# A twelve-layer decoder on one core: one transfer for the maxima of half a sequence, and another order and two queues for the rows of the last softmax layer

## The chip, the cores and the metric

The kernel runs on one core of one Trainium2 chip. The metric is the device time of one execution in microseconds, as the median of several runs. A core has engines that each work through their own program in order: TensorE (matrix products; its weight loads are listed apart, as PEld), VectorE (DVE), ScalarE (ACT), GpSimd (POOL) and SyncE (SP), which here only issues transfers. ScalarE and GpSimd can issue transfers too. Engines wait for each other through semaphores; a wait holds everything that stands behind it in that engine's program.

## The reference

The model has four blocks of three layers over x of 8 sequences, 256 positions and 128 features. Each layer is `x = x + f(layernorm(x))`. Softmax attention with 16 heads of 8 features is f in five layers: L0_attn and L1_attn (causal self-attention with rotary positions), L0_xattn and L1_xattn (cross-attention to a context, with masks) and L3_xattn (cross-attention, no mask). The other layers are three mixtures of experts with sorted tokens (L0, L1, L2), channel attention and retention (L2), a state-space scan (L3_attn) and a latent mixture (L3_ffn). The last block, cut:

```python
def _L3_xattn_ref(query, key, value, Wq, bq, Wk, bk, Wv, bv, Wo, bo):
    Q = proj(query, Wq, bq, Sq)          # (8, 16 heads, 256, 8)
    K = proj(key, Wk, bk, Skv)
    V = proj(value, Wv, bv, Skv)
    scores = jnp.einsum('bhqd,bhkd->bhqk', Q, K) / SCALE
    attn = jax.nn.softmax(scores, axis=-1)
    out = jnp.einsum('bhqk,bhkd->bhqd', attn, V)
    ...
    return jnp.einsum('bsd,ed->bse', out, Wo) + bo
...
x = x + _L2_ffn_ref(_layernorm(x, axis=-1), ...)      # experts
x = x + _L3_attn_ref(_layernorm(x, axis=-1), ...)     # state space
x = x + _L3_xattn_ref(_layernorm(x, axis=-1), ctx_1024, ctx_1024, ...)
x = x + _L3_ffn_ref(_layernorm(x, axis=-1), ...)
```

The query of L3_xattn comes from the norm of x; its key and value come from the context, which is there from the start.

## The kernel before

**Two passes of softmax.** A job is one sequence in one softmax layer: 8 sequences x 5 layers, 40 jobs. Pass 1 (`pass1`) multiplies q by k with q's positions on the partitions, 512 columns at a time, and VectorE takes the negative maximum over k (`neg`, line 824). Pass 2 (`pass2`) multiplies again with k's positions on the partitions, ScalarE takes the exponential (`prob`, line 901), and TensorE multiplies by v (`av`, line 873). The maximum is subtracted inside the second product: q's operand has three extra rows that hold it, against rows of ones in k's operand.

**Rows of q and k.** `qs` and `ks` are the operands, [128 rows, 16 heads, 2 sequences x 256 positions] in bf16, two buffers each, one for even and one for odd pairs of sequences. Each fp32 value of q and k is split on GpSimd into three bf16 pieces (`pieces`, lines 647 and 651: cast, subtract, cast, subtract), and all nine products of pieces are contracted: 72 rows. `spread` (lines 655 to 664) writes them with nine transfers per operand (line 661), for each piece three, every one 8 rows of 16 KB, 128 KB. The destination's rows take the 128 partitions of the piece, head by head. `queues` lists the issuing engines: transfer r of a piece goes to queue r modulo their number; with one queue, the generator yields an estimated 2 us after each piece. Only the first pair of the whole kernel uses two queues, SyncE and ScalarE.

**Fronts.** `front` (lines 673 to 752) prepares a pair of sequences: k's projection from the context (cross-attention), wait for the layer before, norm, transposes, q's projection, a wait for pass 2 of the two jobs that used the same buffers two pairs ago (`before`), then k's rows, q's rows, and v. The first wait, at line 678, takes only the first of these two jobs.

**Maxima.** At the end of half a job (8 heads) GpSimd splits `neg` into three pieces `mp` [128 positions, 2 tiles, 3 pieces, 8 heads] (lines 831 to 834). `all_maxima` (lines 838 to 855) transposes this in one matmul to 48 rows of 128 positions, ScalarE copies them to `mT`, and two transfers, one per tile of 128 positions, write 24 rows each into q's three extra rows (line 852). Pass 2 of this half waits for both.

**Order.** All stages are Python generators. `drive` advances pass 1 and pass 2 job by job, and the others (`fronts`, `all_maxima`, `backs`, the expert and scan layers, called aside) when their estimated due time comes; `yield us(t)` gives such an estimate, and a generator that waits for a key in `done` is passed over. What comes out is one fixed program per engine. So a changed estimate or a changed wait can also move other instructions. SyncE's program holds the row transfers, the maxima's transfers, the expert weights (`r_w`, line 1432, 592 KB each), the sorted tokens (lines 1439 and 1467) and the output.

**Around the last softmax layer.** The experts of L2_ffn for the second half of the batch (lines 1462, 1492, 1495, 1497) run while L3_xattn begins on the first half. When they are done, the scan (L3_attn, lines 1611 to 1767) runs on the second half beside L3_xattn of the first; then L3_xattn of the second half runs beside L3_ffn. The layer object `L3x` is L3_xattn; its jobs are the last eight, pairs 0 and 1 the first half, 2 and 3 the second.

Of the kernel before, what the change touches and what calls it, by code (L numbers as in the profile page):

```python
# [11 lines left out]
BF16 = mybir.dt.bfloat16  # L12
# [6 lines left out]
P = 128  # L19
B = 8  # L20
S = 256
T = S // P
D = 128
H = 16
# [5 lines left out]
KM = P - NPC  # L30
# [217 lines left out]
def kernel(  # L248
# [11 lines left out]
    nc = tc.nc  # L260
# [18 lines left out]
    def sb(shape, tag, bufs, dt=F32):  # L279
        return pools["soft"].tile(list(shape), dt, tag=tag, name=tag, bufs=bufs)  # L280
# [29 lines left out]
    def mm_tile(dt=F32):  # L310

        spare[1] += 1
        if spare[0] and spare[1] % 2:
            return ps_s1.tile([P, 512], dt, tag="s1", name="s1")
        return ps_mm.tile([P, 512], dt, tag="mm", name="mm")
# [6 lines left out]
    def bc(ap, axis, n):  # L322

        a = ap.unsqueeze(axis)
        shape = list(a.shape)
        shape[axis] = n
        return a.to_broadcast(shape)
# [10 lines left out]
    def us(t):  # L338
        return t / TICK
# [3 lines left out]
    def wait(*keys):  # L343
        while not done.issuperset(keys):
            yield BLOCKED
# [118 lines left out]
    identb = cpool.tile([P, P], BF16, name="identb")  # L464
# [16 lines left out]
    qss = [cpool.tile([P, H, 2 * S], BF16, name=f"qs{i}") for i in range(2)]  # L481
    kss = [cpool.tile([P, H, 2 * S], BF16, name=f"ks{i}") for i in range(2)]
# [27 lines left out]
    rt_at, n = {}, 0  # L510
# [68 lines left out]
    def layernorm(dst, src, n):  # L579

        st = sb_all([P, n, 6], "ln_st", 8)
        mv = sb_all([P, n, 2], "ln_mv", 8)
        rs = sb_all([P, n], "ln_rs", 8)
        for i in range(n):
            nc.vector.bn_stats(st[:, i, :], src[:, i, :])
            nc.vector.bn_aggr(mv[:, i, :], st[:, i, :])
        inv_root(rs, mv[:, :, 1], n, 1e-5)
        yield us(5)
        for i in range(n):
            one = nc.vector.tensor_scalar(  # L590
                dst[:, i, :], src[:, i, :], mv[:, i, 0:1], rs[:, i : i + 1], ALU.subtract, ALU.mult)
        last.setdefault("dve", one)
        yield us(2.5)
# [41 lines left out]
    def main_line(jobs, loads, aside):  # L635
# [5 lines left out]
        def pieces(src, nm):  # L641

            out, rest = [], src
            for i in range(NPC):
                if i:
                    r = sb([P, 2 * S], "qkf", 3) if i < NPC - 1 else sb([P, 2 * S], f"pc{i}", 2, BF16)
                    nc.gpsimd.tensor_tensor(r, rest, out[-1], ALU.subtract)
                    rest = r
                if i < NPC - 1:
                    b = sb([P, 2 * S], f"pc{i}", 2, BF16)  # L650
                    nc.gpsimd.tensor_copy(b, rest)  # L651
                    out.append(b)
            return out + [rest]

        def spread(dst, pcs, of_q, queues):


            for a, t in enumerate(pcs):
                for r in range(NPC):
                    at = a * NPC + r if of_q else r * NPC + a  # L660
                    queues[r % len(queues)].dma_start(  # L661
                        dst[at : KR : NPC * NPC].rearrange("d h c -> d (h c)"), t)
                if len(queues) == 1:
                    yield us(2)
# [8 lines left out]
        def front(j, y, b):  # L673
            p = b // 2
            if y is L3x:
                yield from wait("L3x")
            before = [("p2", i) for i in (j - 4, j - 3) if i >= 0]
            yield from wait(("w", y.step), ("rows", p % 2), *before[:1])
            if y.w is None:
                y.w = loaded[y.step]  # L680
                if not y.rope:
                    y.bqs = sb([P, 1], "bqs", 2)
                    nc.vector.tensor_scalar(y.bqs, y.w["bq"], scale, None, ALU.mult)
            w = y.w

            def rows_of(n, src):
                f = sb([P, 2 * S], "qkf", 3)
                if y.rope:
                    parts = []
                    for sw, tab in (("", "cos"), ("s", "sin")):  # L690
                        pp = mm_tile()
                        mm(pp, w["w" + n + sw], src, start=True, stop=True)
                        o = sb([P, 2, S], "probw", 4)
                        pv = pp.rearrange("p (b s) -> p b s", b=2)
                        table = bc(rope[tab + n], 1, 2)
                        if "b" + n in w:
                            nc.vector.scalar_tensor_tensor(o, pv, w["b" + n + sw], table, ALU.add, ALU.mult)
                        else:
                            nc.vector.tensor_tensor(o, pv, table, ALU.mult)
                        parts.append(o)  # L700
                        yield us(1)
                    nc.gpsimd.tensor_tensor(
                        f.rearrange("p (b s) -> p b s", b=2), parts[0], parts[1], ALU.add)
                else:
                    pp = mm_tile()
                    mm(pp, w["w" + n], src, start=True, stop=True)
                    if n == "q":
                        nc.scalar.activation(f, pp, AF.Identity, bias=y.bqs, scale=scale)
                    else:
                        nc.scalar.activation(f, pp, AF.Identity, bias=w["bk"])  # L710
                    yield us(1)
                return pieces(f, n)

            first = j == 0
            if y.cross:
                yield from wait(("ctx", p))
                kp = yield from rows_of("k", ctxP[p])
            yield from wait(*y.needs(p))
            x = xp[p]
            xn = sb([P, 2 * T, D], "xn", 1)  # L720
            yield from layernorm(xn, x, 2 * T)
            xnT = sb([P, 2 * S], "xnT", 1)
            one = transpose_to(xnT, xn, 2 * T, nc.scalar.copy)
            if first:
                last["act"] = one
            yield
            if not y.cross:
                kp = yield from rows_of("k", xnT)
                if first:
                    yield from spread(kss[p % 2], kp, False, (nc.sync, nc.scalar))  # L730
            qp = yield from rows_of("q", xnT)
            if "bo" in w:
                nc.gpsimd.tensor_tensor(x, x, bc(w["bo"], 1, 2 * T), ALU.add)
            yield from wait(*before)
            if not first:
                yield from spread(kss[p % 2], kp, False, (nc.sync,))
            yield from spread(qss[p % 2], qp, True, (nc.sync, nc.scalar) if first else (nc.sync,))
            yield us(1)
            kvT = ctxP[p] if y.cross else xnT
            for i in range(2):  # L740
                pv = mm_tile()
                for t in range(T):
                    at = i * S + t * P
                    mm(pv[:, t * D : (t + 1) * D], kvT[:, at : at + P], w["wv"], start=True, stop=True)
                v = vpads[(2 * p + i) % 4]
                for t in range(T):
                    v_in = pv[:, t * D : (t + 1) * D].rearrange("p (h d) -> p h d", h=H)
                    if "bv" in w:
                        nc.vector.tensor_tensor(v[:, t, :, 0:DK], v_in, w.grid("bv", H), ALU.add)
                    else:  # L750
                        nc.vector.tensor_copy(v[:, t, :, 0:DK], v_in)
                yield us(3)
# [85 lines left out]
        def all_maxima():  # L838

            n = NPC * H // 2  # L840
            for j in range(len(jobs)):
                for half in range(2):
                    yield from wait(("mp", j, half))
                    yield us(3.5)
                    mp, q, h0, c0 = maxima.pop(0)
                    pm = mmb_tile()
                    nc.tensor.transpose(pm[: T * n, :P], mp.rearrange("p t r h -> p (t r h)"), identb)
                    mT = sb([T * n, P], "mT", 2, BF16)
                    nc.scalar.copy(mT, pm[: T * n, :P])
                    for t in range(T):  # L850
                        qt = c0 + t * P
                        nc.sync.dma_start(
                            q[KM:, h0 : h0 + H // 2, qt : qt + P], mT[t * n : (t + 1) * n])
                    done.add(("max", j, half))
                    yield 0

# [920 lines left out]
    L3x = Layer("L3_xattn", pair_of("L3_attn"), cross=True)  # L1777
# [70 lines left out]
```

## Time and profile before

| | |
|---|---|
| runs, us | 1732.77, 1742.9, 1731.68; median 1732.77 |
| profiled execution | 1729.58 us, span 1727.8 us |
| TensorE busy | 1435.5 us (83%), 10546 matmuls |
| TensorE's weight loads | 894.7 us (52%) |
| VectorE busy | 952.3 us (55%) |
| ScalarE busy | 615.9 us (36%) |
| GpSimd busy | 608.6 us (35%) |
| TensorE's mean granted clock | 0.914 |
| chain that ended last, by engine | PE 57%, POOL 11%, DVE 11%, issue 8%, DMA 7%, ACT 3%, SPq 2% |

The span runs from the first to the last instruction of the profiled execution. Busy times of engines overlap, so they don't add up to the span. The chain is followed back from the last instruction, at each step to what released it; "issue" in it is time in which an engine waited for nothing that the profile shows, SPq is SyncE's queue. Lines L1 to L1847 are those of the kernel before. TensorE's clock is granted by a throttle and is given as a share of full speed.

The page lists the transfers that the change touches: `ks<-pc` and `qs<-pc` with 177 issues each of 128 KB on SyncE and three each on ScalarE, and `qs<-mT` with 160 issues of 6 KB on SyncE.

### The profile page before, as it was taken

What the parts mean: (1) busy time and instruction counts of PE and PEld (TensorE: products, weight loads), DVE (VectorE), ACT (ScalarE), POOL (GpSimd) and SP (SyncE); (2) the same over time, 40 slices, a digit from 0 to 9 for tenths busy, and PEclk for the clock granted to TensorE, in tenths of its full rate; (3) what the DMA queues carried; (4) which work ended last, traced back from release to release, by engine and by line L of the source; (5) the groups of instructions that cost most, each with busy time, mean ns of one, the idle gap of its engine ahead of it and who ended that gap; (6) DMA issues with size and microseconds to landing.
All of it is one profiled execution on the core that took longest, in us unless ns stands there. A gap on an engine that the chain in (4) does not pass through costs nothing.

```text
span 1727.8 us, 28942 instructions
## 1 busy us (share of the span) xinstructions
PE 1435.5 (83%) x10546; PEld 894.7 (52%) x10546; DVE 952.3 (55%) x2546; ACT 615.9 (36%) x1267; POOL 608.6 (35%) x859
## 2 busy tenths in 40 slices
PE   3897898888799778889989899567967787988997
PEld 1454454566345456545556566356744563554553
DVE  5445776636467553656544455313367355757753
ACT  0352343441333343234443345112322224533551
POOL 3424656412565441252331322312134523342211
PEclk7899999999999899999999999679978888998996
DMA  3332111344201226211245300147400452012000
GB/s 106 90 111 61 40 57 30 112 142 136 72 24 47 66 80 192 89 57 57 58 137 179 113 28 2 57 151 240 146 15 25 148 158 82 11 53 78 8 8 13
DMA packets 113519, 141.64 MB, mean 82 GB/s; under 512 B 12384, under 2 KB 97888, under 8 KB 113248
## 3 DMA queue, kind: packets, MB, share of 16 engines
q1 hardware_dynamic: 94064, 121.33, 22.4%
q10 hardware_dynamic: 16240, 12.17, 2.4%
q0 software_dynamic: 3072, 6.30, 1.1%
q8 instruction: 83, 1.36, 0.3%
q14 instruction: 60, 0.49, 0.1%
HBM read 79.53 MB, written 12.06 MB: 53 GB/s over the span
## 4 chain that ended last, share of the span: by engine, by line
PE 57%; POOL 11%; DVE 11%; issue 8%; DMA 7%; ACT 3%; SPq 2%; another core or an unknown queue 0%; POOLq 0%; ACTq 0%; DVEq 0%
PE av L873 9%; PE sc L1492 6%; PE s L815 6%; PE sc L893 6%; DVE neg L824 4%; PE mm L1462 3%; DMA qs<-pc 2%; PE s L821 2%; PE sc L898 2%; POOL probw L906 2%; SPq L661 2%; POOL r_x L1514 2%; POOL xsorted L1409 2%; PE mm L502 2%; DMA r_w<-in_w_L_big_dram 2%
## 5 line engine op out<-in xcount | busy, mean ns | idle before, releaser
L824 DVE TENSOR_REDUCE neg<-s 128x2 f32<-128x512 f32 (+1 forms) x576 | 387.1, 683 | 217.3 <-PE s L818 78.3
L901 ACT ACTIVATE prob<-sc 128x512 f32<-128x512 f32 x576 | 336.2, 597 | 379.2 <-PE sc L898 196.8
L815 PE MATMUL s<-ks,qs 125*128 125x256 bf16 (+1 forms) x1280 | 236.4, 274 | 89.6 <-DVE neg L824 56.2
L893 PE MATMUL sc<-qs,ks 128*128 128x256 bf16 (+1 forms) x1280 | 227.7, 269 | 4.6 <-DMA qs<-mT 4.3
L815 PEld LDWEIGHTS <-qs 125*128 125x128 bf16 x1280 | 113.5, 102 | 197.5 <-issue 154.4
L1492 PE MATMUL sc<-r_xT,r_w 128*128 128x128 f32 x720 | 166.1, 323 | 46.6 <-ACT r_h L1495 13.8
L873 PE MATMUL av<-prob,vpad 128*32 128x256 f32 (+1 forms) x2048 | 168.3, 368 | 15.9 <-issue 9.8
L1492 PEld LDWEIGHTS sc<-r_xT,r_w 128*128 128x128 f32 x720 | 115.2, 203 | 98.3 <-ACT r_h L1495 44.9
L893 PEld LDWEIGHTS <-ks 128*128 128x128 bf16 x1280 | 110.8, 100 | 97.4 <-issue 65.2
L1497 DVE TENSOR_SCALAR r_h<-sc,r_w 128x128 f32<-128x128 f32 x180 | 62.6, 349 | 157.7 <-PE sc L1492 156.2
L1495 ACT ACTIVATE r_h<-sc,r_w 128x128 f32<-128x128 f32 x180 | 66.1, 368 | 171.6 <-PE sc L1492 143.1
L651 POOL CAST pc<-qkf 128x512 bf16<-128x512 f32 x80 | 51.8, 648 | 209.7 <-ACT qkf L710 148.7
L1462 PE MATMUL mm<-r_w,r_h 128*128 128x128 f32 x600 | 106.9, 292 | 0.8 <-DVE r_h L1497 0.7
L906 POOL TENSOR_TENSOR probw<-prob,sideT 128x512 f32<-128x512 f32 x64 | 84.3, 1318 | 48.7 <-ACT prob L901 48.4
L831 POOL CAST mp<-neg 128x16 bf16<-128x16 f32 x80 | 19.8, 247 | 222.1 <-DVE neg L824 205.7
L1462 PEld LDWEIGHTS mm<-r_w,r_h 128*128 128x128 f32 x600 | 88.7, 203 | 7.4 <-DVE r_h L1497 2.4
L873 PEld LDWEIGHTS av<-prob,vpad 128*32 128x32 f32 x2048 | 47.0, 108 | 87.1 <-issue 55.6
L577 POOL TENSOR_TENSOR ln_rs<-ln_rs,nhalf 128x4 f32<-128x4 f32 x40 | 43.3, 1085 | 131.0 <-DVE ln_rs L576 130.3
L878 ACT COPY avs<-av 128x512 f32<-128x512 f32 x80 | 46.9, 586 | 82.6 <-PE av L873 60.8
L1514 POOL DMA_INDIRECT r_x<-ysorted,r_sloti x48 | 46.5, 970 | 74.6 <-PE s L1477 59.9
L873 PE MATMUL av<-probw,vpad 128*32 128x256 f32 x512 | 53.0, 399 | 23.6 <-POOL probw L906 23.4
L906 DVE TENSOR_TENSOR probw<-prob,sideT 128x512 f32<-128x512 f32 x64 | 56.2, 878 | 27.6 <-ACT prob L901 18.1
(408 smaller groups left out, 2579.0 us busy)
## 6 DMA issues: line engine op xcount, KB each, us to landing
r_w<-in_w_L_big_dram SPq DMA_DIRECT2D x60, 578.0 KB
ks<-pc SPq DMA_DIRECT2D x177, 128.0 KB
qs<-pc SPq DMA_DIRECT2D x177, 128.0 KB
r_w<-in_w_L_big_dram SPq DMA_DIRECT2D x30, 579.0 KB
r_x<-xsorted SPq DMA_DIRECT2D x18, 256.0 KB
ysorted<-r_y SPq DMA_DIRECT2D x18, 256.0 KB
mi<-in_mask_dram ACTq DMA_DIRECT2D x16, 256.0 KB
qs<-mT SPq DMA_DIRECT2D x160, 6.0 KB
```

The source lines that it names most:

```text
L651: nc.gpsimd.tensor_copy(b, rest)
L815: one = mm(bank[:, a, :], q[:KM, g + a, c0 + qt * P : c0 + (qt + 1) * P], k[:KM, g + a, c0 : c0 + nk], start=a == 0 or y.bare, stop=y.bare)
L824: last["dve"] = nc.vector.tensor_reduce(neg[:, qt, g - h0 : g - h0 + nh], bank, AX.X, ALU.max, negate=True)
L873: mm(o, sumsel if sums else v[:, at : at + G], probs[j][0 if sums else 1], start=kt == 0 and not sums, stop=kt == T - 1 and sums == (sideT ...
L893: one = mm(bank[:, a, :], k[:, g + a, c0 + kt * P : c0 + (kt + 1) * P], q[:, g + a, c0 + q0 : c0 + S], start=a == 0 or y.bare, stop=y.bare)
L901: last["act"] = nc.scalar.activation(p, bank, AF.Exp)
L906: eng.tensor_tensor(pw, p, bc(sideT[:, kt, :], 1, nh), ALU.mult)
L1462: mm(py, hid[:, f, :], wt[:, w2 : w2 + D], start=f == 0, stop=f == NF - 1)
L1492: mm(o, wt[:, f * P : (f + 1) * P], xT[:, i, :], start=True, stop=True)
L1495: nc.scalar.activation(hid[:, f, :], o, AF.Relu, bias=bias)
L1497: nc.vector.tensor_scalar(hid[:, f, :], o, bias, 0.0, ALU.add, ALU.max)
L1514: nc.gpsimd.indirect_dma_start(yg[:, i, :], None, ysort, bass.IndirectOffsetOnAxis(ap=sloti[:, at : at + 1], axis=0))
```

## The change

For the maxima, `mp` is transposed in two matmuls, one per tile of 128 positions, side by side into the same bank: 24 rows of 256 positions instead of 48 rows of 128. ScalarE copies 24 x 256, and one transfer writes all 256 positions into q's three extra rows.

For L3x, k's rows are spread right after k's projection, ahead of the wait for the layer before and of the norm; the wait for both earlier pass 2's (`before`) comes ahead of this, so also ahead of the norm. And k's and q's rows of L3x go by two queues: of three transfers per piece, two on SyncE and one on ScalarE. With two queues `spread` gives no estimates between pieces.

```diff
             first = j == 0
+            queues = (nc.sync, nc.scalar) if first or y is L3x else (nc.sync,)
             if y.cross:
                 yield from wait(("ctx", p))
                 kp = yield from rows_of("k", ctxP[p])
+                if y is L3x:
+                    yield from wait(*before)
+                    yield from spread(kss[p % 2], kp, False, queues)
             yield from wait(*y.needs(p))
...
             yield from wait(*before)
-            if not first:
-                yield from spread(kss[p % 2], kp, False, (nc.sync,))
-            yield from spread(qss[p % 2], qp, True, (nc.sync, nc.scalar) if first else (nc.sync,))
+            if not first and y is not L3x:
+                yield from spread(kss[p % 2], kp, False, queues)
+            yield from spread(qss[p % 2], qp, True, queues)
...
                     mp, q, h0, c0 = maxima.pop(0)
                     pm = mmb_tile()
-                    nc.tensor.transpose(pm[: T * n, :P], mp.rearrange("p t r h -> p (t r h)"), identb)
-                    mT = sb([T * n, P], "mT", 2, BF16)
-                    nc.scalar.copy(mT, pm[: T * n, :P])
                     for t in range(T):
-                        qt = c0 + t * P
-                        nc.sync.dma_start(
-                            q[KM:, h0 : h0 + H // 2, qt : qt + P], mT[t * n : (t + 1) * n])
+                        nc.tensor.transpose(
+                            pm[:n, t * P : (t + 1) * P], mp[:, t].rearrange("p r h -> p (r h)"), identb)
+                    mT = sb([n, S], "mT", 2, BF16)
+                    nc.scalar.copy(mT, pm[:n, :S])
+                    nc.sync.dma_start(q[KM:, h0 : h0 + H // 2, c0 : c0 + S], mT)
                     done.add(("max", j, half))
```

In the instruction order of the changed program, as it is built, SyncE has 80 maxima transfers instead of 160, and of L3x's 72 row transfers 48; ScalarE has the other 24. For the first pair of L3x SyncE's program has six transfers of k, then three expert weights, then six of q, then further weights.

## The prediction

> **What bounds the kernel now.** I read the page first: TensorE is busy 1435.5 us of a span of 1727.8 (83%) and carries 57% of the chain that ended last. So a change counts either by TensorE work on that chain or by a stretch in which TensorE stands. I looked for such stretches with the busy time by stretch (columns: stretch, its us, then busy us and instructions of PE, PEld, DVE, ACT, POOL, then granted clock, DMA share, GB/s).
>
> ```profile
> 1355.00:1376.00 21.00, 18.52 (x120) 14.47 (x118) 8.69 (x24) 7.22 (x17) 9.54 (x11) 1.00 0.52 158
> 1376.00:1398.00 22.00, 12.20 (x52) 9.97 (x51) 3.58 (x12) 2.06 (x5) 0.00 (x0) 0.69 0.62 176
> 1397.00:1428.00 31.00, 27.44 (x179) 21.20 (x180) 23.40 (x58) 8.40 (x21) 10.91 (x19) 0.94 0.47 152
> 1428.00:1455.00 27.00, 16.68 (x132) 8.04 (x131) 12.54 (x32) 11.69 (x25) 10.40 (x20) 0.81 0.37 114
> 1455.00:1533.00 78.00, 75.79 (x586) 44.13 (x584) 56.69 (x148) 47.16 (x98) 23.36 (x35) 1.00 0.06 17
> 1533.00:1549.00 16.00, 12.15 (x63) 8.29 (x63) 7.88 (x25) 4.09 (x8) 11.82 (x16) 1.00 0.25 75
> 1570.00:1678.00 108.00, 106.49 (x756) 56.90 (x757) 72.44 (x220) 59.04 (x113) 21.41 (x39) 0.98 0.08 25
> ```
>
> In 1376 to 1398 TensorE idles 9.8 us, its clock is 0.69 and GpSimd does nothing: transfers bound this stretch. In 1455 to 1533 and from 1570 on TensorE is 97% and 99% busy: there only work counts. The chain of waits names the transfer (start, us, what):
>
> ```profile
> 1375.60 0.61 SPq L661
> 1376.31 9.27 DMA qs<-pc
> 1385.60 11.38 DMA qs<-pc
> 1396.98 0.72 issue
> ```
>
> The first pass 1 of L3x starts at 1397.70, when its q rows are in. SyncE's timeline shows why they are late (columns: start, us, queue, line, what, count):
>
> ```profile
> 1359.12 0.77 SPq L661 DMA_DIRECT2D ks<-pc  x1
> 1363.56 4.13 SPq L1432 DMA_DIRECT2D r_w<-in_w_L_big_dram  x3
> 1367.73 3.57 SPq L661 DMA_DIRECT2D ks<-pc  x5
> 1374.27 1.94 SPq L661 DMA_DIRECT2D ks<-pc  x3
> 1376.31 2.47 SPq L661 DMA_DIRECT2D qs<-pc  x3
> 1381.11 6.53 SPq L661 DMA_DIRECT2D qs<-pc  x6
> ```
>
> One k transfer goes out, three expert weights block the queue until 1367.7, eight k transfers follow, and only then q, whose pieces GpSimd had finished at 1372.9. The maxima's rows by their tile (ns min/median/max):
>
> ```profile
> L852 SPq DMA_DIRECT2D qs<-mT x160: 697/722/832, 48.7 to 1662.1; - x160
> L849 ACT COPY mT<-mm x80: 243/254/262, 48.4 to 1661.0; 48x128 bf16<-48x128 bf16 x80
> L847 PEld LDWEIGHTS <-mp x80: 98/99/115, 48.1 to 1660.3; 128*48 128x48 bf16 x80
> L847 PE MATMUL mm<-identb,mp x80: 216/237/303, 48.1 to 1660.3; 128*48 128x128 bf16 x80
> ```
>
> The sum is made against this execution: 1729.58 us, 1.8 of them around the span. It lies 0.2% under the median of the runs, 1732.77; I add the result to the median.
>
> **The change, part by part.**
>
> The maxima, 80 halves (8 sequences, 5 layers, 2 halves). (a) 80 SyncE issues of 0.72 us go, 58 us of queue time; almost all of it lies beside SyncE's waits for the copy itself (356 us for ScalarE's mT in the queue's waits). On the chain, followed stretch by stretch, the landing of a maxima transfer stands three times (2.17, 2.97, 4.62 us), each right behind the first issue of its pair, so it is the second transfer that is awaited; 3 x 0.72 = 2.2 us are saved; ends: 0, and 8 x 0.72 = 5.8 for the eight places where the issue itself is on the chain. What is late next there is the copy, which I cost below. (b) 80 transposes are added on TensorE. The trace has no second one behind a first; one takes 0.17 us from its start to the next instruction (1427.33 to 1427.50), its weight load 0.099. I take 0.11, near the weight load, since back-to-back bf16 matmuls of this kernel start 0.11 apart. L847 lies on the chain at 54 of its 80 places: 54 x 0.11 = +5.9; ends: 0, if TensorE would wait for something else anyway, and 54 x 0.17 = 9.2. (c) The copy goes from 48x128 at 0.254 to 24x256; the nearest row, a 128x256 copy on ScalarE, takes 0.37. That is 80 x 0.116 = 9.3 us of ScalarE, which carries 3% of the chain: +0.3, covered by an engine busy 36%; uncovered it would be 9.3. Together +4.0.
>
> L3x, four pairs of sequences, 18 row transfers each. (d) The k rows of the first pair now stand in SyncE's order ahead of the three weights, six on SyncE and three on ScalarE's queue; q's six and three follow these weights with nothing of k between. Nothing of k leaves between 1367.7 and 1376.2, so q can go as its pieces appear, from 1369.8. The 9.8 us of idling in 1376 to 1398 consist of two waits for weights (3.66 and 3.93), 0.96 for q and small ones. I let one weight wait remain: the three weights now go after k's third piece (1363.4 and two issues, 1.1 us later than 1363.56) and behind eight more transfers of 128 KB (1.05 MB at that stretch's 158 GB/s, 6.6 us). So 9.8 - 3.7 = 6.1 saved; ends 0 (bytes bound it) and 9.8. (e) The clock was 0.69 there against 0.94 in the stretch behind; at 0.9 the 12.2 us of work would take 9.4: 2.8 saved, and 0 at the other end. Late next are the experts: in the changed order 74 pass-1 matmuls, 18 of pass 2 and 12 value matmuls stand ahead of the last expert matmul, against 48, 4 and 0. The experts' end hardly moves; the gain is cashed in 1455 to 1533, which has less softmax work left.
>
> (f) ScalarE now issues 24 transfers. The first of each three waits for GpSimd's first piece, the last for its third, so ScalarE's queue is held from cast to last subtraction: 3.75 us for q (1369.11 to 1372.86), 4.92 for k (1358.46 to 1363.38), plus 0.62 per issue. Behind it stand the experts' r_h in the first pair, for which TensorE waits in program order, and ss_m in the third. I charge one hold of the first pair less what the remaining weight wait absorbs, +3; ends: 0, and 8 holds of 4.3, 35 us. In the second pair 42 pass-1 matmuls stand in a row beside the holds: 21 reductions of 0.68 on VectorE, 14 us of cover; without it, two holds, 8.6 us. (g) The new wait for both earlier pass 2's ahead of the norm costs nothing for pairs 0 and 1, whose buffers are long free, nor for pair 2, where q's projection stood behind all of pass 2 already (128 of 128 matmuls before and after); its cover gone, it would be one norm and projection, 1525.8 to 1535.3, 9.5 us. (h) From pair 2 on, moving three issues of 0.61 off SyncE saves at most 1.8 of q's last landing, and by the rows below 0.2; I take 1.2. Against that, four scan groups that ran while q was on its way (1535 to 1545) now stand behind pass-1 matmuls; VectorE bounds pass 1 there (18.8 of 21 us in 1549 to 1570), so TensorE has gaps for them: +1.5, ends 0 and all of their matmuls, 6.5 (four times 1.1 and two value steps of 1.05). Together -6.1 - 2.8 + 3 - 1.2 + 1.5 = -5.6.
>
> The trace has both forms of (h): nine q transfers by two queues at the start took 10.4 us from first issue to last landing (26.94 to 37.3), by one queue in pair 2 10.6 (1537.96 to 1548.6); both are paced by GpSimd's pieces. The Trainium skill, page "DMA: Bandwidth & Descriptors", section "Issuing engines are not separate DMA queues", speaks against the edit: transfers from any engine end on the same 16 DMA engines, so a second issuer saves issue time alone. By it (h) would be 1.8 and the sum -2.2; by the rows' difference, 0.2, it would be -0.6.
>
> The other softmax layers keep their row order but for a few neighbours. Sum: 4.0 - 5.6 = -1.6, so 1729.58 becomes 1728.0 and the median 1731; I say 1730.
>
> **The rivals.**
>
> Rows really early (20%). q lands by about 1384, 1378 for the last issue after the holds plus six of landing as in the 4.5 to 6.6 us rows of calmer stretches. Pass 1 starts 13.7 us earlier, and all of it arrives at the end; with (h) at 1.8 and the maxima at -2.2 + 0.3 (transposes hidden) that is -17.4: 1715. For: 9.8 us of idling and GpSimd at 0.00. Against: the order puts 26 pass-1 matmuls more ahead of the experts, and pair 2 waits for the scan, not for pass 1.
>
> Bytes bound it (20%). The weights and rows of 1355 to 1398 are the same bytes on the same engines; DMA share 0.52 and 0.62 speaks against, waits for weights on TensorE for. Then (d) and (e) go: -1.6 + 8.9 = +7.3: 1740.
>
> Slower: ScalarE held (15%). One mechanism, (f): ScalarE's in-order queue waits for GpSimd at eight places; six have no pass-1 cover, 6 x 4.3 = 26 in place of 3. With the rest -4.6 that gives +21: 1754. It decides from the point where more than about three holds are uncovered. For: the r_h and ss_m right behind. Against: ScalarE did 2.06 us in 1376 to 1398.
>
> The change not doing what it says: both parts stand in the built order, 80 maxima transfers for 160 and k ahead of the weights; I leave that out.
>
> **How the numbers follow.** My forecast has 45%, 1722 to 1738 by (a) to (c). About 1% is what a measurement here tells from no change, 17 us. Faster by it: most of the first rival and the forecast's tail, 0.17. Slower: the last rival, and a tail of the bytes' case, 0.15. Within: 0.68. The range takes in the first rival's 1715 less 2 and most of the slow one: 1713 to 1750.
>
> **What would show it.** Right: the q landing at 1376 to 1397 gone from the chain, ks issued in one run ahead of three weights, TensorE's idling in that stretch under 5 us; 80 maxima transfers, the copy near 0.37, two L847-type transposes about 0.11 apart; TensorE busy up 8 to 14 us by transposes. Wrong: r_h or ss_m waiting 4 us behind ScalarE's issues, an L3x that starts pass 1 at 1394 or later, or a shift of several us ahead of 1340, where only the maxima part acts and I allow +3.

## The result, and the profile after

The changed kernel takes 1763.33 us in the median of four runs (1753.69 to 1766.64), the kernel before 1734.02 (1731.68 to 1742.9). The ratio is 1.0142, with a 95% interval from 1.0109 to 1.0176: 19 to 31 us slower, where 1730 was forecast and 1750 was the upper end of the range. The span of the profiled execution is 1760.5 us against 1727.8.

Up to L3x the changed kernel is ahead: ScalarE copies the first k projection of L3x (`qkf`, line 710) at 1351.7 us against 1357.6. (In the fourteen traces that have the new maxima part this point lies between 1345.0 and 1357.6 us, so a lead of 5.9 is within the scatter.) All of the loss lies behind this point: from there to the end of the span the changed kernel takes 408.8 us, the kernel before 370.2. The busy time by stretch, for the stretches shown of before and one more (stretch, its us; busy us and instructions of PE, PEld, DVE, ACT, POOL; granted clock, DMA share, GB/s):

```profile
1355.00:1376.00 21.00, 12.94 (x68) 11.21 (x69) 3.47 (x11) 4.94 (x12) 5.92 (x7) 0.79 0.53 167
1376.00:1398.00 22.00, 17.84 (x109) 14.68 (x109) 13.38 (x40) 4.69 (x12) 5.86 (x10) 0.89 0.56 180
1397.00:1428.00 31.00, 21.60 (x96) 14.66 (x96) 17.64 (x33) 4.09 (x10) 7.44 (x19) 0.68 0.37 113
1428.00:1455.00 27.00, 25.84 (x209) 16.77 (x212) 8.89 (x25) 14.38 (x31) 3.93 (x4) 0.99 0.35 101
1455.00:1533.00 78.00, 68.50 (x468) 37.30 (x462) 49.57 (x126) 41.67 (x85) 23.07 (x39) 0.89 0.10 30
...
1551.00:1567.00 16.00, 5.12 (x22) 2.79 (x21) 3.11 (x12) 1.37 (x2) 7.21 (x9) 0.73 0.42 122
1570.00:1678.00 108.00, 97.23 (x634) 56.16 (x632) 76.50 (x220) 43.88 (x85) 26.32 (x51) 0.91 0.08 27
```

The windows stand at the same times in both kernels, though the changed one is 5.9 us further on in its work. The stretch that the change aims at, 1376 to 1398, idles 4.2 us on TensorE instead of 9.8. But the stretch ahead of it idles 8.1 instead of 2.5, the one behind it 9.4 instead of 3.6, with 96 matmuls instead of 179 and a clock of 0.68 instead of 0.94. And at 1551 there is a hole of 11 us.

**First place, the experts.** ScalarE's timeline (start, us, engine or queue, line, what, count; in brackets the idle time ahead and what ended it):

```profile
1353.23 4.89 ACTq L661 DMA_DIRECT2D ks<-pc  x3
1358.18 0.62 ACT L1498 ACTIVATE r_h<-sc,r_w 128x128 f32<-128x128 f32 x2 [5.28 <-DMA ks<-pc]
...
1370.36 3.76 ACTq L661 DMA_DIRECT2D qs<-pc  x3
1374.30 0.62 ACT L1498 ACTIVATE r_h<-sc,r_w 128x128 f32<-128x128 f32 x2 [4.64 <-DMA qs<-pc]
...
1414.36 0.37 ACT L1498 ACTIVATE r_h<-sc,r_w 128x128 f32<-128x128 f32 x1 [14.33 <-PE sc L1495]
```

Three issues hold ScalarE's queue for 4.89 and 3.76 us, since each stands until GpSimd has its piece, and `r_h` of the experts comes behind them. The last line is another matter: there ScalarE waits 14.33 us for an expert matmul. TensorE's timeline shows the first hold, and then what stands ahead of that matmul:

```profile
1358.60 0.80 PE L1495 MATMUL sc<-r_xT,r_w 128*128 128x128 f32 x2 [4.71 <-ACT r_h L1498]
...
1409.13 1.18 PE L819 MATMUL s<-ks,qs 125*128 125x256 bf16 x4 [0.24 <-DVE neg L828]
1410.49 1.19 PE L819 MATMUL s<-ks,qs 125*128 125x256 bf16 x4 [0.18 <-DVE neg L828]
1411.86 1.18 PE L819 MATMUL s<-ks,qs 125*128 125x256 bf16 x4 [0.18 <-DVE neg L828]
1412.84 0.63 PE L1495 MATMUL sc<-r_xT,r_w 128*128 128x128 f32 x2
```

From 1399.2 on, 42 pass-1 matmuls stand in a row, paced by VectorE's reductions (two matmuls per 0.68 us), and the expert comes behind the last. The last tokens leave the experts at 1447.14 us: 95.4 us behind k's projection, where it was 70.7.

**Second place, the scan of pair 3.** TensorE's timeline again, and then VectorE's and GpSimd's:

```profile
1553.75 1.10 PE L706 MATMUL mm<-ctxT,w 128*128 128x512 f32 x2
1565.36 1.01 PE L819 MATMUL s<-ks,qs 125*128 125x256 bf16 x4 [10.51 <-DMA ks<-pc]
1566.73 1.26 PE L819 MATMUL s<-ks,qs 125*128 125x256 bf16 x4 [0.35 <-DVE neg L828]
1567.83 1.22 PE L1740 MATMUL sc<-ss_u,w_L_tables 128*128 128x256 f32 x2
```

```profile
1565.98 0.69 DVE L828 TENSOR_REDUCE neg<-s 128x2 f32<-128x512 f32 x1 [11.66 <-PE s L819]
1566.59 0.16 DVE L1687 TENSOR_TENSOR ss_da<-ss_dt,ss_a 128x8 f32<-128x8 f32 x1
```

```profile
1566.85 2.99 POOL L1737 TENSOR_SCALAR ss_u<-w_L_tables,ss_da 128x256 f32<-128x256 f32 x4 [5.51 <-DVE ss_da L1687]
```

TensorE stands 10.51 us for pair 2's rows, because pass 1 is next in its program. The scan needs no rows. But its `ss_da`, 0.16 us of work, stands on VectorE behind the first reduction of that pass 1, `ss_u` on GpSimd waits for `ss_da`, and the scan's matmuls for `ss_u`. In the kernel before, these groups ran while the rows travelled, up to the start of pass 1 (TensorE's timeline of the kernel before; L1737 and L815 are there what L1740 and L819 are here):

```profile
1543.40 0.70 PE L1737 MATMUL sc<-ss_u,w_L_tables 128*128 128x256 f32 x2 [0.21 <-POOL ss_u L1734]
...
1549.07 0.60 PE L815 MATMUL s<-ks,qs 125*128 125x256 bf16 x4 [1.91 <-DMA qs<-pc]
```

The last `ss_m` of the scan comes 45.3 us behind the q projection of pair 2 instead of 10.8.

**The maxima** by their tile (ns min/median/max):

```profile
L855 ACT COPY mT<-mm x80: 344/357/362, 50.2 to 1685.2; 24x256 bf16<-24x256 bf16 x80
L856 SPq DMA_DIRECT2D qs<-mT x80: 697/752/837, 50.6 to 1685.5; - x80
```

The copy is at 0.357 us (forecast: 0.37), and one issue of 0.752 us stands for two of 0.722.

### The profile page after: what moved, and what is told of

Same layout as the page of the kernel before. It is cut to its first block, busy times and chain, and to the rows that moved or that the text cites. A ratio compares the mean times of both kernels' runs of the same rounds, so it can differ in the third digit from the quotient of the medians.

```text
span 1760.5 us, 28993 instructions
## 1 busy us (share of the span) xinstructions
PE 1450.8 (82%) x10626; PEld 900.6 (51%) x10626; DVE 952.4 (54%) x2546; ACT 626.2 (36%) x1267; POOL 606.5 (34%) x859
## 2 busy tenths in 40 slices
DMA packets 111359, 141.65 MB, mean 80 GB/s; under 512 B 8304, under 2 KB 95728, under 8 KB 111088
## 4 chain that ended last, share of the span: by engine, by line
PE 58%; DVE 12%; POOL 11%; issue 8%; DMA 7%; ACT 3%; SPq 1%; another core or an unknown queue 0%; ACTq 0%; POOLq 0%; DVEq 0%
PE av L876 9%; PE sc L1495 6%; PE sc L896 6%; PE s L819 6%; DVE neg L828 5%; PE mm L1465 3%; DMA qs<-pc 3%; PE sc L901 2%; PE s L825 2%; POOL probw L909 2%; PE mm L502 2%; POOL r_x L1517 2%; PE mm L936 2%; PE mm L620 1%; POOL xsorted L1412 1%
## 5 line engine op out<-in xcount | busy, mean ns | idle before, releaser
L819 PE MATMUL s<-ks,qs 125*128 125x256 bf16 (+1 forms) x1280 | 241.0, 278 | 113.3 <-DVE neg L828 69.4
L819 PEld LDWEIGHTS <-qs 125*128 125x128 bf16 x1280 | 116.0, 103 | 225.8 <-issue 184.6
L876 PE MATMUL av<-prob,vpad 128*32 128x256 f32 (+1 forms) x2048 | 174.5, 372 | 7.1 <-ACT prob L904 6.7
```

Source lines behind the costliest of these rows:

```text
L819: one = mm(bank[:, a, :], q[:KM, g + a, c0 + qt * P : c0 + (qt + 1) * P], k[:KM, g + a, c0 : c0 + nk], start=a == 0 or y.bare, stop=y.bare)
L876: mm(o, sumsel if sums else v[:, at : at + G], probs[j][0 if sums else 1], start=kt == 0 and not sums, stop=kt == T - 1 and sums == (sideT ...
```

## The experiments

Fifteen runs beside the two kernels; the changed kernel heads the table. The ratio is against runs of the kernel before on the same chip, with its 95% interval. The two columns behind come from one profiled execution each: from k's first projection in L3x to the last tokens of the experts (first place), and from pair 2's q projection to the last `ss_m` of the scan (second place). The kernel before has 70.7 and 10.8.

| run | ratio | experts' end, us | last ss_m, us |
|---|---|---|---|
| changed kernel | 1.0142 [1.0109, 1.0176] | 95.4 | 45.3 |
| max_alone | 0.9915 [0.9889, 0.9941] | 69.7 | 10.8 |
| max_alone_again | 0.9918 [0.9882, 0.9955] | 70.9 | 10.8 |
| two_transposes_two_transfers | 1.0015 [0.9986, 1.0043] | 65.1 | 10.8 |
| l3x_rows_alone | 1.0206 [1.0149, 1.0262] | 96.7 | 45.1 |
| one_queue | 1.0037 [1.0011, 1.0064] | 76.9 | 19.6 |
| two_queues_alone | 1.0016 [0.9991, 1.0041] | 78.0 | 8.1 |
| no_estimates_alone | 1.0073 [1.0047, 1.0099] | 85.2 | 36.2 |
| scalar_with_estimates | 1.0113 [1.0074, 1.0151] | 77.2 | 24.7 |
| no_scalar_same_order | 1.0067 [1.0036, 1.0098] | 84.1 | 44.0 |
| pairs_0_1 | 1.0049 [1.0026, 1.0073] | 97.0 | 11.7 |
| pairs_0_1_sync_only | 0.9962 [0.9938, 0.9985] | 81.0 | 11.5 |
| pairs_2_3 | 1.0119 [1.0079, 1.0160] | 69.9 | 44.8 |
| pairs_2_3_sync_only | 1.0073 [1.0050, 1.0097] | 71.8 | 45.8 |
| pairs_2_3_scan_first | 1.0058 [1.0026, 1.0089] | 65.4 | 18.3 |
| changed_scan_first | 1.0176 [1.0121, 1.0232] | 95.6 | 15.3 |

0.01 of the ratio is 17 us. From the two intervals, the difference of two runs is uncertain by some 6 to 9 us. The runs from one_queue on have the maxima part of the change in full, so their base is max_alone, not the kernel before.

**The maxima part.** max_alone is the kernel before with the second half of the diff alone; two_transposes_two_transfers leaves the two transfers:

```diff
-                    nc.sync.dma_start(q[KM:, h0 : h0 + H // 2, c0 : c0 + S], mT)
+                    for t in range(T):
+                        qt = c0 + t * P
+                        nc.sync.dma_start(
+                            q[KM:, h0 : h0 + H // 2, qt : qt + P], mT[:, t * P : (t + 1) * P])
```

> The kernel before with the maxima part alone (two transposes, one copy of 24x256, one transfer). The prediction's steps (a) to (c) say +4.0 us against the kernel before. The trace of the changed kernel, where the events ahead of the last softmax layer come 5.9 us earlier than before, says -4 to -7 us, with TensorE busier by some 10 to 15 us all the same. If that lead is drift between two executions, it is -1 to +1.

> The kernel before with the two transposes and the 24x256 copy, but still two transfers for the maxima of half a sequence: steps (b) and (c) without step (a). The prediction's terms (b) and (c) say +6.2 us against the kernel before. If the added transposes lie in time that TensorE would wait anyway, 0 to +2; then the maxima part's -15 us is the missing second transfer's (or the changed order's, since the instruction order here is nearly that of before).

> The kernel before with the rows part of the change alone, the maxima as before. If the two parts add up: 1.0142 / 0.9915 = 1.023, +34 to +44 us against the kernel before. If the maxima part's gain is had only in the order of the kernel before, or most of it is a happy order: +22 to +30.

> The maxima part alone once more, as the base on this chip: 0.989 to 0.994 of the kernel before, as in the first run of it.

max_alone is 15 us faster than the kernel before (10 to 19), more than any of the three expectations, and the second time 14. It is the fastest kernel here, ahead of both. With two transfers nothing of that is left: 1.0015, so the transposes and the copy cost -2 to +7 us, and the step from two transfers to one gives some 17. This step also makes the rows 512 bytes instead of 256 (packets under 512 bytes: 12384 with two transfers, 8304 with one); no run separates the size of the packets from the number of transfers. TensorE's waits that the profile puts down to the maxima's rows, of the kernel before, of two_transposes_two_transfers and of max_alone, in this order (what waits for what: us, times, longest):

```profile
PE s L815 <- DMA qs<-mT: 6.9, 3, 3.7
...
PE sc L893 <- DMA qs<-mT: 4.3, 1, 4.3
```

```profile
PE s L815 <- DMA qs<-mT: 5.8, 2, 4.1
...
PE sc L895 <- DMA qs<-mT: 4.1, 1, 4.1
```

```profile
PE s L815 <- issue: 3.2, 3, 1.9
PE sc L892 <- DMA qs<-mT: 3.1, 1, 3.1
```

These are 11.2 and 9.9 us against 3.1. But two of the places still wait in max_alone, only under `issue`: 0.63 us where the kernel before waits 1.35 (at 309.8 us) and 1.93 where it waits 3.67 (at 599.2). So 5.7 us are left, and 4 to 6 us of the gain are shorter waits of this kind. Where the rest is, the waits do not say. Some of it seems to lie ahead of L3x: k's first projection there comes at 1357.6, 1365.3 and 1364.9 us in the three traces with two transfers, at 1345.0 to 1357.6 in the fourteen with one. The instruction order of max_alone also differs a little (45 pass-1 and 8 pass-2 matmuls ahead of the last expert matmul, before 48 and 4, with two transfers again 48 and 4). The two parts add up: 1.0206 x 0.9915 = 1.012, within the interval of the changed kernel.

**Order, ScalarE or k's place.** Three theories for the rows part: 1, the instruction order, which comes from the missing estimates; 2, ScalarE held by its own issues; 3, k ahead of the norm. Each run takes something back from the changed kernel:

```diff
 # no_scalar_same_order: all on SyncE, no estimates
-            queues = (nc.sync, nc.scalar) if first or y is L3x else (nc.sync,)
+            queues = (nc.sync, nc.scalar) if first else (nc.sync,)
...
-                if len(queues) == 1:
+                if not rush:
                     yield us(2)
...
 # scalar_with_estimates: two queues, with estimates
-                if len(queues) == 1:
+                if paced:
                     yield us(2)
...
 # one_queue: SyncE, with estimates, k ahead
-            queues = (nc.sync, nc.scalar) if first or y is L3x else (nc.sync,)
+            queues = (nc.sync, nc.scalar) if first else (nc.sync,)
```

`rush` is true for L3x's rows and the first pair's, `paced` false for the first pair alone.

> The changed kernel with all row transfers of L3x on SyncE, still without estimates between pieces, so that the instruction order stays almost that of the changed kernel (74 pass-1, 18 pass-2 and 12 value matmuls ahead of the last expert matmul) and ScalarE issues nothing. Theory 1 (the order costs it: pass 1 stands ahead of the experts and of the scan): still +20 to +33 us against the kernel before. Theory 2 (ScalarE is held by its own 24 issues): back to -8 to +5. Theory 3 (k's rows ahead of norm and weights cost it): +20 to +33.

> The changed kernel with both queues, but with the estimate of 2 us after each piece also with two queues; 64 pass-1, no pass-2 and no value matmul then stand ahead of the last expert matmul. ScalarE keeps its 24 issues. Theory 1 (order): -10 to +8 us against the kernel before. Theory 2 (ScalarE held): +20 to +33. Theory 3 (k's place): +20 to +33.

> The changed kernel with L3x's rows by SyncE alone and with the estimates, k's rows still ahead of the norm and of the weights. Theory 1 (order, which comes from the missing estimates): -10 to +5 us against the kernel before. Theory 2 (ScalarE held): -8 to +3. Theory 3 (k's place): +20 to +33.

No theory holds alone. no_scalar_same_order lies at +12 us, between what 1 and 2 said; scalar_with_estimates at +20, where 1 said +8 at most; one_queue at +6, where 3 said +20. Measured from max_alone, one_queue, k ahead with the estimates kept, costs 21 us (1.0037 / 0.9915 = 1.012). TensorE's timeline of one_queue shows what became of its early rows:

```profile
1364.73 0.80 PE L1495 MATMUL sc<-r_xT,r_w 128*128 128x128 f32 x2 [4.68 <-DMA r_w<-in_w_L_big_dram]
...
1371.52 0.27 PE L502 MATMUL mm<-ident,xn 128*128 128x128 f32 x1
...
1373.40 1.13 PE L706 MATMUL mm<-xnT,w 128*128 128x512 f32 x2
```

Nine k transfers go ahead of the expert weights, and an expert waits 4.68 us for these weights; the front's norm, transposes and q projection come behind that expert in TensorE's program. q's projection is 23.8 us behind k's, in max_alone 10.7, and pass 1 starts only 1.3 us earlier against k's projection (37.9 for 39.2). It is the estimates of k's pieces, now ahead of the norm, that push q's projection back: in no_scalar_same_order, with k ahead and everything on SyncE but without estimates, it is 10.7 us behind k's and pass 1 starts at 27.7. Where one_queue's 21 us are is not shown by this. All its waits for weights from here to the end are 6.1 us, in max_alone 7.3. Its order differs too: 64 pass-1 matmuls stand ahead of the last expert matmul, 40 of them in a row (max_alone: 45, at most 8 in a row).

**The other two edits alone**, on max_alone, k in its old place (the line for q's rows is changed in the same way):

```diff
 # two_queues_alone, with estimates
-                yield from spread(kss[p % 2], kp, False, (nc.sync,))
+                yield from spread(kss[p % 2], kp, False, (nc.sync, nc.scalar) if y is L3x else (nc.sync,))
...
 # no_estimates_alone, all on SyncE
-                yield from spread(kss[p % 2], kp, False, (nc.sync,))
+                yield from spread(kss[p % 2], kp, False, (nc.sync,), y is not L3x)
```

> The maxima part, and L3x's rows by SyncE and ScalarE with the estimate after each piece; k's rows in their old place behind the norm. The two runs with k ahead and estimates, by one and by two queues, lie 13 us apart; if ScalarE's holds cost that by themselves, this is +9 to +17 us against the maxima part alone (-6 to +2 against before). If they only cost where k goes ahead: -2 to +4 (-17 to -11 against before).

> The maxima part, k's rows in their old place, all on SyncE, but L3x's rows without estimates between pieces. 74 pass-1, 18 pass-2 and 12 value matmuls stand ahead of the last expert matmul, 178 pass-1 matmuls ahead of the last scan work (146 with estimates). If this order is the main cause of the loss: +15 to +30 us against the maxima part alone (0 to +15 against before). If k's earlier place is the main cause: 0 to +7 (-15 to -8 against before).

Two queues alone: 17 us above max_alone, the upper end of the first expectation. No estimates alone: 27 us, and the table shows it in both places (85.2 and 36.2) with k's place and ScalarE untouched: the order is a cause by itself. Each of the three edits costs 17 to 27 us alone and all together 39, so their costs do not add up. two_queues_alone is late in the first place alone (78.0; second place 8.1). Its 17 us are not holds like those above: with the estimates ScalarE's issues go out mostly one at a time, and TensorE's waits for `r_h` from L3x's start to the end are 4.9 us against 3.3 in max_alone. Where they are stays open.

**Which half.** New rows for two of the four pairs:

```diff
+            new = y is L3x and p < 2        # pairs_2_3: p >= 2
-            queues = (nc.sync, nc.scalar) if first or y is L3x else (nc.sync,)
+            queues = (nc.sync, nc.scalar) if first or new else (nc.sync,)
...
-                if y is L3x:
+                if new:
...
-            if not first and y is not L3x:
+            if not first and not new:
```

> The changed kernel with L3x's new rows (k ahead, two queues, no estimates) for pairs 0 and 1 alone; pairs 2 and 3 as in the kernel before. In the trace of the changed kernel the experts end 19 us later than before; 74 pass-1 matmuls stand ahead of the last expert matmul here too. If that delay reaches the end, this is +15 to +20 us against the maxima part alone (0 to +5 against the kernel before); if the stretch behind it, in which TensorE is busy all the time, takes it back because less softmax work is left, it is 0 to +8 (-15 to -7 against before).

> The changed kernel with L3x's new rows for pairs 2 and 3 alone. Experts end as in the kernel before. Theory 1 in its second place (pass 1 of pair 2 stands in TensorE's program ahead of scan groups that need no rows, so TensorE idles while the rows are on their way): +15 to +30 us against the maxima part alone (0 to +15 against before). If only the experts' half costs: 0 to +5 against the maxima part alone (-15 to -10 against before).

pairs_0_1 loses 23 us on max_alone, and its last two columns are the changed kernel's in the first place and max_alone's in the second; for pairs_2_3, which loses 35, it is the other way round. The two places are separate, and the delay of the experts is not taken back behind them: in pairs_0_1's trace pair 2's q projection, the scan and the end all lie 17 to 19 us behind max_alone. The times do not add up here either: 23 and 35 are 58 us, and the changed kernel loses 39.

**ScalarE's share in each place.** The same halves, without estimates, all on SyncE:

> New rows for pairs 0 and 1 alone as in the run pairs_0_1, without estimates and with almost its instruction order (74 pass-1, 18 pass-2 and 12 value matmuls ahead of the last expert matmul), but all on SyncE. In the run with two queues TensorE waits 13.8 us for ScalarE's r_h in L3x's part, with the maxima part alone 3.3. If ScalarE's holds are that part of the first place: r_h waits fall to 3 to 5 us and the time is 9 to 13 us under pairs_0_1; the order's own part, 10 to 14 us above the maxima part alone, stays. If the order is everything: within 4 us of pairs_0_1.

> New rows for pairs 2 and 3 alone as in the run pairs_2_3, without estimates, but all on SyncE. The last scan group's ss_m came 31 us later there than with the maxima part alone, and 31 us later too with k in its old place and all on SyncE without estimates; so if the missing estimates alone make the second place, this is within 6 us of pairs_2_3. If ScalarE's issues have a part in it: 10 to 20 us under pairs_2_3.

First place: 1.0049 goes to 0.9962, 15 us, a little more than expected, and the experts' end from 97.0 to 81.0. TensorE's waits from 1350 to 1455 us, first of pairs_0_1, then of pairs_0_1_sync_only:

```profile
PE sc L1496 <- ACT r_h L1499: 13.8, 5, 5.6
PE s L820 <- DVE neg L829: 4.5, 13, 1.2
```

```profile
PE s L820 <- DVE neg L829: 6.0, 16, 1.6
PE sc L1496 <- DMA r_w<-in_w_L_big_dram: 3.9, 2, 3.3
...
PE sc L1496 <- ACT r_h L1499: 1.5, 3, 0.5
```

The waits for `r_h` go, a long row of pass-1 matmuls ahead of the experts stays (36 in a row, with two queues 42), and the time is still 8 us over max_alone (0.9962 against 0.9915). That the order costs these 8 us is argued and not shown. In the second place the ss_m column does not move (44.8, 45.8); the ratio falls by 0.0046, which was expected at most 6 us and is 8, with intervals that meet. Whether ScalarE's issues have a small part there stays open.

**Putting the scan ahead.** One wait more at the head of `pass1`, to move the order in the second place alone:

```diff
             yield from wait(("front", j // 2 * 2), ("terms", j))
+            if y is L3x and b == 4:
+                yield from wait(("L3_attn", 3))
```

> The run with the new rows for pairs 2 and 3 alone, with one wait more in the generator: pass 1 of the first job of pair 2 starts when the scan of pair 3 has been put out. ScalarE's issues, the missing estimates, k ahead of the norm all stay; 144 pass-1 matmuls instead of 192 stand ahead of the last scan work. Theory 1 (scan groups stand behind pass 1, which waits for rows): 18 to 32 us of that run's loss go, which is -12 to +3 us against the kernel before. Theory 2 (ScalarE's holds, or the wait ahead of the norm): it stays at +12 to +25.

> The changed kernel with the same one wait. Theory 1 with two places (experts in the first half, scan in the second): only the first place is left, so it lands near the run with new rows for pairs 0 and 1 alone, 0 to +14 us against the kernel before. Theory 2: +20 to +30 as the changed kernel.

On pairs_2_3 it takes back 0.0061, 11 us, less than the 18 to 32 of theory 1, and the scan is nearly in its old place (18.3). On the changed kernel it also puts the scan right (15.3), but the time stays at 1.0176, +30 us: theory 1 missed, and theory 2's number was met. The maxima of the first job of pair 2 come 34.0 us behind the q projection there, in the changed kernel 27.9, in max_alone 24.1. Put all of the scan first, and pass 1 is late; put pass 1 first, and the scan is late. But this does not explain the miss: in pairs_2_3_scan_first the maxima come 35.3 us behind, in pairs_2_3 27.1, and there the wait gained 11 us. Why the changed kernel gains nothing by it stays open.

## Why the prediction was wrong, by its own steps

**(a) to (c), the maxima: right mechanism, a term mis-sized.** (a) was -2.2 with an end of -5.8; one transfer for two gave 17. At the three places that the step found on the chain TensorE's wait fell by 1.2, 0.7 and 1.7 us, 3.6 in all, where it charged 0.72 each. The larger part of the 17 lies outside these places, and the runs do not say where. (b) and (c), +6.2, lie inside what was measured, -2 to +7, and so does zero. In the changed kernel TensorE's busy time rose by 15.3 us, where 8 to 14 were to be the transposes'; but with the maxima part alone it fell by 8.2 (1427.3 after 1435.5), so the rise is not theirs. Two transposes start 0.06 apart, not 0.11 (max_alone: 1462.16 and 1462.22).

**(d), k ahead of the weights: the rows came early, and it did not pay.** The first pass 1 starts 32.5 us behind k's projection instead of 40.1: 7.6 of the 8.9 us that (d) and (e) promised for this stretch. q's landing is gone from the chain there, and one landing of weights is left on it (3.70 us from 1390.93). The step moved the transfers and forgot that a front is one sequence: what k's rows bring with them ahead of the norm, ScalarE's holds here and the estimates in one_queue, puts the norm later (q's projection is 17.2 us behind k's, in one_queue 23.8, before 10.7). And where nothing is put later, early rows do not pay either: in pairs_0_1_sync_only q's projection is 10.7 us behind k's and pass 1 starts at 24.5, 15 us earlier than in max_alone, and the kernel is 8 us slower than max_alone.

**(e) failed in "The experts' end hardly moves".** It moved by 24.7 us, and the gain could not be cashed behind it. The counts were there (74, 18 and 12 matmuls ahead of the last expert against 48, 4 and 0), and were read as softmax work already done, not as work that the experts stand behind.

**(f) failed in its +3.** ScalarE's holds cost 15 us in pairs 0 and 1 (pairs_0_1 against pairs_0_1_sync_only). The holds are as long as taken from the profile, 3.8 to 4.9 us. The cover was wrong: 42 pass-1 matmuls in a row do keep TensorE in work, but the experts, which wait for ScalarE, come behind them as well, so hold and cover are paid one after the other: the second pair's holds lie at 1393.4 to 1397.1 and 1419.8 to 1423.6, the row of 42 between them, at 1399.2 to 1412.8. The rival "ScalarE held" had the holds right, and 1754; it did not have the order, so that its number came nearest is in part luck. It took the holds ahead of `ss_m` for as dear as those ahead of `r_h`; for these the runs show 8 us, with intervals that meet.

**(g), the wait ahead of the norm, 0:** not tried alone, so it stays open.

**(h) failed in "TensorE has gaps for them" and +1.5.** The displaced scan groups did not run in gaps between pass-1 matmuls; they stood behind matmuls that waited for rows. no_estimates_alone has it with neither ScalarE nor k's place touched (36.2 us to the last `ss_m`), pairs_2_3 pays 35 us on max_alone. The step priced the groups' own matmuls, 6.5 us at most, and not the wait of what they were put behind.

**Bytes bound it** is out: pass 1 did start early. **Rows really early** was right in its premise and wrong in that it arrives at the end.

**Idling and the clock.** From 6 us ahead of k's first projection to the last output transfer, max_alone takes 365.3 us and the changed kernel 410.7. By windows of 3 us, TensorE's idling grew from 44.8 to 62.8 us, and what its busy time lost to the granted clock (busy time less busy time x clock) from 20.3 to 42.3. The rest, 5.4 us, is work. So beside 18 us of idling up to 22 more went to the clock, which no step of the prediction charged. "Up to", since a slower matmul costs nothing where another engine sets the pace: 4.8 us of the 42.3 lie at 1398.0 to 1412.8, where VectorE does (busy 3.72 of 4 us at 1408 to 1412). And the two do not go together everywhere. two_queues_alone has 4.8 us more idling than max_alone and 11.0 more lost to the clock, pairs_0_1_sync_only 1.7 us less idling and 6.3 more lost to the clock, and changed_scan_first 7.5 us less idling than the changed kernel and 5.2 more lost to the clock. These are single executions (max_alone_again: 45.1 and 21.7); what lowers the clock in these orders is not shown. The busy time by stretch of the changed kernel, around both places (columns as above):

```profile
1555.00:1565.00 10.00, 0.00 (x0) 0.00 (x0) 0.00 (x0) 0.69 (x1) 4.66 (x5) 0.67 0.53 158
1565.00:1568.00 3.00, 2.20 (x9) 1.10 (x10) 2.01 (x4) 0.00 (x0) 1.15 (x2) 0.50 0.56 138
...
1574.00:1577.00 3.00, 2.91 (x12) 2.19 (x11) 1.48 (x3) 0.49 (x1) 1.47 (x4) 0.50 0.00 0
...
1408.00:1412.00 4.00, 3.35 (x13) 1.38 (x12) 3.72 (x7) 0.00 (x0) 0.83 (x4) 0.50 0.00 0
1412.00:1415.00 3.00, 2.98 (x15) 2.62 (x14) 1.96 (x4) 0.37 (x1) 0.00 (x0) 0.50 0.00 0
```

Behind the 10.51 us of idling the clock is 0.50 for 12 us. The Trainium skill, page "TensorE: Matmul & The Clock Gate", "Part 1: The HAM clock gate (the "warmup" mystery)", has it so that an idle window of about 3.4 us halves the clock and a busy one of the same length restores it. The trace agrees with the halving; the way back took more than three such windows here, with TensorE busy in 9.9 of the 12 us.

## What to carry to other kernels

Where programs are in order and written out ahead, a transfer that is issued earlier also moves what its generator does next, and a dropped estimate moves whatever the scheduler weighs against it: count what stands behind each moved instruction on every engine, down to a VectorE operation of 0.16 us. Work put "in front" is cover only for a wait that is not itself queued behind that work. Take a change of two parts apart before judging it: here one part gains 15 us and the other loses some 36.

## What was not expected of the hardware

The clock fell to 0.50 without any long idling: at 1408 to 1412 TensorE is busy 3.35 of 4 us and waits 0.18 to 0.24 us at a time for VectorE's reductions, and still has half its clock, until 1415. In max_alone, where pass 1 is mixed with experts, the clock from 1404 to 1416 is 1.00 with 3.14 to 3.85 us busy in each 4. Why the one is slowed and the other not stays open. And a second issuing engine is not free: ScalarE was held for 3.8 to 4.9 us by three issues of 0.62, since an issue that waits for its source holds everything behind it. In pairs 0 and 1 this cost 15 us (pairs_0_1 against pairs_0_1_sync_only). The Trainium skill's page "DMA: Bandwidth & Descriptors", which the prediction cites and by which a second issuer saves issue time alone, speaks of the saving. two_queues_alone lost 17 us without such long holds, and what it lost them to stays open.
